# First cross attention of a two-layer decoder: rotation and values partly moved to ScalarE and GpSimd, gate and places made for pairs of batches

## The chip, the cores and the metric

The kernel runs on one core of a Trainium2 chip. The metric is the device time of one execution in microseconds. The engines are named as in the profile: PE (TensorE matmul) and PEld (its weight loads), DVE (VectorE), ACT (ScalarE), POOL (GpSimd), SP (SyncE, which here issues DMAs).

## The reference

A decoder of two layers with a layer norm after each of six parts works on `x` of shape (16, 128, 256), float32:

```python
x = ln(x + L0_attn(x));  x = ln(x + L0_xattn(x, ctx));  x = ln(x + L0_ffn(x))
x = ln(x + L1_attn(x));  x = ln(x + L1_xattn(x, ctx, ctx)); x = ln(x + L1_ffn(x))
```

The change lies in the second part, `L0_xattn`, and in the gate that leads to the third. The cross attention treats the 128 rows as channels and the 256 columns as positions, with 16 heads of 8 channels, of which 4 are rotated by position:

```python
q = rope(wq @ x + bq);  k = rope(wk @ c + bk);  v = wv @ c + bv      # per head
p = softmax(q @ k.T / sqrt(8));  out = wo @ (p @ v) + bo
```

The third part is a mixture of 8 experts, of which each row takes the two best:

```python
w = softmax(x @ Wg + bg);  topv, topi = top_k(w, 2)
out = sum over the two of topv * expert[topi](x)    # three matrix products, gelu between
```

## The kernel before

All of `x` stays in SBUF as 16 tiles `x_t[b]` of 128x256, one per batch. The ternary self attention (`ternary`) and the first cross attention (`rope_cross_plain`) form one stream, which `by_beats` writes out by hand. The cross attention has 8 beats per batch. In each beat PE makes a group of scores for the maxima (of one batch) and a group of transposed scores for the exponentials (of an earlier batch, 11 beats behind); then come the products with the values two beats later, and then the jobs of the beat. Where a job stands relative to its batch is in the list `jobs` as a number of beats.

What sets the order of the work: PE's instructions are kept in the order in which the program writes them (`mm` and `turned`, L216 to L222). On the other engines a scheduler chooses the order when the program is built, and each engine then runs its list in that order. So an engine that waits for one thing holds up all that stands behind it in its list.

Buffers in PSUM: the scores `ps_st` have three buffers in turn, the sums `ps_o` one, and everything else shares one buffer `ps_m` once the ternary attention has ended. Each `ps_st` for the maxima goes into the buffer that the last exponential (`pT`, L443 on ACT) has read.

A batch in the cross attention, by its jobs and lines:

- `keys` and `queries` (beats -8 and -5): PE makes two products into `ps_m`, the plain one and the one for the rotation. `rotated` (L766) makes `rot` (L770) and `rot_t` (L771) on DVE and adds them on POOL (L772). For the queries POOL then makes four masked copies `z` (L858).
- `values` (beat 5): two products, and DVE adds the bias `bv2` while it spreads them into `v8` (L871).
- maxima: DVE reduces the scores (`nm`, L438); the job `maxima` (beat 9) turns them on PE.
- `divide` (beat 20, L319 to L325): ACT copies the sums to `ol`, DVE shuffles the row sums into place (`l`, L322), ACT takes Ln and Exp for the reciprocal (L323, L324), DVE multiplies (L325).
- `finish` (beat 23): output product, bias and residual (L841), and the layer norm `normalised`, whose `rstd` is a power on POOL (L195).
- `gate_turn`, `gate`, `places` (beats 25, 26, 28): PE turns `x_t[b]` (L222), ACT copies it (`gate_xT`, L782); the gate's product, softmax, the two best (DVE, ACT); from these the place of each row in its experts' lists (counts so far in `free`), and two scatters of `x_t[b]` to `xs` in device memory by indirect DMA on POOL's queue (L831).

The experts (`experts_by_place`) then read `xs` in order, on SP's queue (`xe<-xs`, L943).

Of the kernel before, what the change touches and what calls it, by code (L numbers as in the profile page):

```python
# [9 lines left out]
F32 = mybir.dt.float32  # L10
# [19 lines left out]
def kernel(ctx: ExitStack, tc: tile.TileContext, a: dict, out: bass.AP):  # L30
# [11 lines left out]
    def load(pool, shape, src, name, dtype=F32, eng=None):  # L42
        t = pool.tile(shape, dtype, name=name)
        (eng or nc.sync).dma_start(t, src)
        return t
# [105 lines left out]


    xw = load(cpool, [P, 8, P], a["xw"], "xw", eng=nc.gpsimd)
    xb = load(cpool, [P, 5], a["xb"], "xb", eng=nc.gpsimd)
    bv2 = load(cpool, [P, D], a["bv2"].partition_broadcast(P), "bv2", eng=nc.gpsimd)
    rope = load(cpool, [P, 2, D], a["rope"], "rope", eng=nc.gpsimd)
    ctx_t = [load(cpool, [P, D], a["ctx"][b], f"ctx_{b}", eng=nc.gpsimd) for b in range(B)]
# [59 lines left out]
    def mm(*args, **kw):  # L217

        tc.keep_in_program_order(nc.tensor.matmul(*args, **kw))  # L219
# [93 lines left out]
        nc.vector.tensor_tensor(oT.rearrange("p c q -> p (c q)"), o[:, 0, :], r, ALU.mult)  # L313
        return oT

    def divided_pairs(pl, o):


        ol = pl["w"].tile([P, 2, D], F32, name="ol")  # L319
        nc.scalar.copy(ol, o)  # L320
        l = pl["w"].tile([P, 2, D], F32, name="l")
        nc.vector.stream_shuffle(l, ol, [n % 16 + 16 for n in range(32)])  # L322
        nc.scalar.activation(l, l, AF.Ln)  # L323
        nc.scalar.activation(l, l, AF.Exp, scale=-1.0)  # L324
        nc.vector.tensor_tensor(l, ol, l, ALU.mult)  # L325
        return l

    def rows_of(g):
        return slice(32 * g, 32 * g + 32)
# [436 lines left out]
    def rotated(pl, pab, n, dst):  # L766

        t0 = pl[dst].tile([P, D], F32, name=f"rot{n}")
        t1 = pl["w"].tile([P, D], F32, name="rot_t")
        nc.vector.scalar_tensor_tensor(t0, pab[:, 0, :], xb[:, 2 * n : 2 * n + 1], rope[:, 0, :], ALU.add, ALU.mult)  # L770
        nc.vector.scalar_tensor_tensor(t1, pab[:, 1, :], xb[:, 2 * n + 1 : 2 * n + 2], rope[:, 1, :], ALU.add, ALU.mult)  # L771
        nc.gpsimd.tensor_tensor(t0, t0, t1, ALU.add)  # L772
        return t0

# [2 lines left out]
    def gate_turn(pl, b):  # L777
        pt = pl["m"].tile([P, 2, P], F32, name="ps_m")
        for c in range(2):
            turned(pt[:, c, :], x_t[b][:, c * P : (c + 1) * P], ident)  # L780
        xT = pl["w"].tile([P, 2, P], F32, name="gate_xT")
        nc.scalar.copy(xT, pt)  # L782
        gates[b] = xT

    def gate(pl, b):

        xT = gates[b]
        pg = pl["m"].tile([P, 8], F32, name="ps_m")
        for c in range(2):
            mm(pg, lhsT=xT[:, c, :], rhs=wg[:, c, :], start=(c == 0), stop=(c == 1))  # L790
        gw = small.tile([P, 8], F32, name="gw")
        nc.vector.tensor_tensor(gw, pg, bg, ALU.add)
        gm = small.tile([P, 1], F32, name="gm")
        nc.vector.tensor_reduce(gm, gw, AX.X, ALU.max, negate=True)
        gs = small.tile([P, 1], F32, name="gs")
        nc.scalar.activation(gw, gw, AF.Exp, bias=gm, accum_out=gs)
        nc.vector.reciprocal(gs, gs)
        nc.vector.tensor_scalar_mul(gw, gw, gs)
        nc.vector.max(gv[:, b, :], gw)
        gi = small.tile([P, 8], U32, name="gi")  # L800
        nc.vector.max_index(gi, gv[:, b, :], gw)
        gf = small.tile([P, 2], F32, name="gf")
        nc.vector.tensor_copy(gf, gi[:, 0:2])
        nc.vector.tensor_tensor(
            oh[:, b], gf.unsqueeze(2).to_broadcast([P, 2, 8]), iota8.unsqueeze(1).to_broadcast([P, 2, 8]), ALU.is_equal
        )
        both = small.tile([P, 8], BF16, name="both")
        nc.vector.tensor_tensor(both, oh[:, b, 0, :], oh[:, b, 1, :], ALU.add)
        gates[b] = gf, both

    def places(pl, b):

        gf, both = gates.pop(b)
        pp = pl["m"].tile([P, 2, 8], F32, name="ps_m")
        mm(pp[:, 0, :], lhsT=above, rhs=both, start=True, stop=True)
        mm(pp[:, 1, :], lhsT=onesb, rhs=both, start=True, stop=True)
        at = small.tile([P, 8], F32, name="at")
        nc.vector.tensor_tensor(at, pp[:, 0, :], free[b % 2], ALU.add)
        nc.vector.tensor_tensor(free[(b + 1) % 2], pp[:, 1, :], free[b % 2], ALU.add)
        own_at = small.tile([P, 2, 8], F32, name="own_at")  # L820
        nc.vector.tensor_tensor(own_at, oh[:, b], at.unsqueeze(1).to_broadcast([P, 2, 8]), ALU.mult)
        pf = small.tile([P, 2], F32, name="place_f")
        nc.vector.tensor_reduce(pf, own_at, AX.X, ALU.add)

        past = small.tile([P, 2], F32, name="past")
        nc.vector.tensor_scalar(past, gf, float(NT - CAP), float(8 * CAP), ALU.mult, ALU.add)
        nc.vector.scalar_tensor_tensor(past, pf, float(CAP), past, ALU.is_ge, ALU.mult)
        nc.vector.scalar_tensor_tensor(pf, gf, float(CAP), pf, ALU.mult, ALU.add)
        nc.vector.tensor_tensor(place[:, b, :], pf, past, ALU.add)
        for n in range(2):  # L830
            nc.gpsimd.indirect_dma_start(  # L831
                out=xs[:, :], out_offset=bass.IndirectOffsetOnAxis(ap=place[:, b, n : n + 1], axis=0), in_=x_t[b],
                in_offset=None,
            )

    def cross_finish(pl, b, *products):
        po = pl["m"].tile([P, D], F32, name="ps_m")
        for n, (w, oT) in enumerate(products):
            mm(po, lhsT=xw[:, w, :], rhs=oT, start=(n == 0), stop=(n == len(products) - 1))
        xn = pl["w"].tile([P, D], F32, name="xn")  # L840
        nc.vector.scalar_tensor_tensor(xn, po, xb[:, 4:5], x_t[b], ALU.add, ALU.add)  # L841
        normalised(x_t[b], xn)

    def rope_cross_plain(pl):

        kept = {}

        def side(b, n, src):
            pab = pl["m"].tile([P, 2, D], F32, name="ps_m")
            for i in range(2):  # L850
                mm(pab[:, i, :], lhsT=xw[:, 2 * n + i, :], rhs=src, start=True, stop=True)
            return rotated(pl, pab, n, "wq"[n])

        def queries(b):
            q = side(b, 0, x_t[b])
            z = pl["q"].tile([P, 4, D], F32, name="z")
            for i in range(4):
                nc.gpsimd.tensor_scalar_mul(z[:, i, :], q, hm[:, 2 + i : 3 + i])  # L858
            kept[b]["qz"] = z

        def keys(b):
            kept[b] = {}
            kept[b]["k"] = side(b, 1, ctx_t[b])

        def values(b):
            pv = pl["m"].tile([P, 2, P], F32, name="ps_m")
            for kc in range(2):
                mm(pv[:, kc, :], lhsT=ctx_t[b][:, kc * P : (kc + 1) * P], rhs=xw[:, 4, :], start=True, stop=True)
            v = kept[b]["v"] = v8[b % 2]
            for n in range(2):  # L870
                nc.vector.tensor_tensor(  # L871
                    v[:, :, n::2, 8 * n : 8 * n + 8],
                    pv.rearrange("p c (g i n d) -> p (c g) i n d", g=4, i=2, n=2)[:, :, :, n, :],
                    bv2.rearrange("p (g i n d) -> p g i n d", g=8, i=2, n=2)[:, :, :, n, :], ALU.add,
                )

        def maxima(b):
            kept[b]["nmT"] = turned_maxima(pl, kept[b]["nm"], nmx[b % 2], 4)

        def divide(b):  # L880
            kept[b] = divided_pairs(pl, kept[b]["o"])

        def finish(b):
            oT = kept.pop(b)
            cross_finish(pl, b, (6, oT[:, 0, :]), (7, oT[:, 1, :]))

        jobs = [(20, divide), (9, maxima), (-8, keys), (-5, queries), (5, values), (23, finish),
                (25, lambda b: gate_turn(pl, b)), (26, lambda b: gate(pl, b)), (28, lambda b: places(pl, b))]
        return 8, 11, cross_scores(pl, 16, kept, 11), jobs, range(B)

    def rope_cross_masked(st):
# [3 lines left out]
        for b in range(B):  # L895
# [16 lines left out]
            v = v8p[b % 2]  # L912
            nc.vector.tensor_copy(own_channels(v, 16), vn.rearrange("p c (h d) -> p c h d", h=16))
            oT = cross_heads(pl, 16, rot[0], [z[:, i, :] for i in range(4)], v, dict(masked, v=vn))
            cross_finish(pl, b, (5, oT.rearrange("p c q -> p (c q)")))
            for part in (gate_turn, gate, places):
                part(pl, b)

# [109 lines left out]


    most1 = const.tile([P, 1], F32, name="most1")  # L1030
    nc.vector.tensor_reduce(most1, free[B % 2], AX.X, ALU.max)
    most_i = const.tile([P, 1], I32, name="most_i")
    nc.vector.tensor_copy(most_i, most1)
    fullest = nc.values_load(most_i[0:1, 0:1], min_val=0, max_val=NT)
# [417 lines left out]
def layouts(inputs):  # L1452
# [20 lines left out]
    for n in range(2):  # L1473
# [9 lines left out]
        "rope": rope.astype(np.float32),  # L1483
        "w0": np.stack([i[f"L0_attn_w_{n}"].T for n in "qkvo"], 1),
        "xw": np.stack([wq.T, wq[mate].T, wk.T, wk[mate].T, wv.T, wo.T] + pairs, 1),
        "xb": np.stack([bq, bq[mate], bk, bk[mate], bo], 1),
        "bv2": np.concatenate([i["L0_xattn_bv"]] * 2),
        "wg": i["L0_ffn_Wg"],
        "bg": i["L0_ffn_bg"],
# [41 lines left out]
```

## Time and profile before

| | |
|---|---|
| median of 3 runs | 1535.75 us (1534.78 to 1538.27) |
| profiled execution, own time | 1539.54 us |
| its span, first to last instruction | 1537.8 us |
| PE busy, PE weight loads | 1372.2 us (89%), 857.4 us (56%) |
| DVE, ACT, POOL busy | 814.4 (53%), 568.0 (37%), 271.6 us (18%) |
| first cross attention alone | from about 200 to 565 us |
| granted TensorE clock, mean | 0.959 |

The times are medians of whole executions; the profile is one execution, and its span is what sums from its rows are held against. Busy time is counted per engine from the records. A matmul's end is modelled, so a busy PE may still have gaps. In a timeline row the first number is the start, the second the duration in us, then engine, line, operation, output and inputs; in brackets stands how long the engine was idle before it and which instruction ended that wait. In a row of waits stand the total in us, how often, and the longest.

### The profile page before, as it was taken

Reading aid. Unit: us, or ns where it says so; the run is one execution under the profiler, and the core shown is the slowest. Engines: PE = TensorE matmul, PEld = TensorE weight load, DVE = VectorE, ACT = ScalarE, POOL = GpSimd, SP = SyncE. Lnnn points to the kernel's source line nnn. Section 1 sums busy time; section 2 is a strip of 40 time slices with the busy share of each in tenths; the row PEclk is TensorE's granted clock in tenths of the full one; section 3 lists DMA queues with packets and bytes.
Section 4 is the critical chain, followed back from the end, with each engine's and each line's share of the span. In section 5 each row is a group of like instructions: output and inputs, shape, how many; then the busy total and the mean of one; then the engine's idle time right before and its main releaser. Section 6 shows DMA issues by size and latency. Waiting matters only on the chain. (4 is left out here: it accounts for less than half of the span.)

```text
span 1537.8 us, 28608 instructions
## 1 busy us (share of the span) xinstructions
PE 1372.2 (89%) x12011; PEld 857.4 (56%) x12011; DVE 814.4 (53%) x2258; ACT 568.0 (37%) x955; POOL 271.6 (18%) x372
## 2 busy tenths in 40 slices
PE   4999989989998949999999679889899998999997
PEld 3666544445444427777777456556455544446666
DVE  6788867777787530000000147766666656542322
ACT  1444334454445512111111124434455554762110
POOL 7000323433333110000000133321122100000000
PEclk9999979999999969999999859989999998999999
DMA  9200000000000025322220411100000000000000
GB/s 298 74 2 2 2 1 8 15 12 12 15 15 12 15 92 168 98 90 89 94 67 18 145 39 29 29 1 2 1 2 1 2 1 1 1 1 12 17 7 20
DMA packets 41743, 58.14 MB, mean 38 GB/s; under 512 B 4752, under 2 KB 31392, under 8 KB 41472
## 3 DMA queue, kind: packets, MB, share of 16 engines
q1 hardware_dynamic: 35984, 41.95, 8.3%
q0 software_dynamic: 4784, 13.42, 2.7%
q8 instruction: 98, 1.61, 0.4%
q10 hardware_dynamic: 832, 0.79, 0.2%
q14 instruction: 45, 0.37, 0.1%
HBM read 39.37 MB, written 16.78 MB: 37 GB/s over the span
## 5 line engine op out<-in xcount | busy, mean ns | idle before, releaser
L438 DVE TENSOR_REDUCE nm<-ps_st 128x4 f32<-128x1024 f32 x192 | 233.7, 1220 | 85.1 <-PE ps_st L219 84.5
L443 ACT ACTIVATE pT<-ps_st 128x1024 f32<-128x1024 f32 x192 | 196.3, 1023 | 212.0 <-PE ps_st L219 212.0
L195 POOL TENSOR_TENSOR rstd<-ve,nhalf 128x1 f32<-128x1 f32 x112 | 62.6, 559 | 681.8 <-DVE ve L194 665.6
L219 PE MATMUL ps_st<-rot,z 32*128 32x256 f32 x1024 | 149.4, 410 | 26.4 <-ACT pT L443 24.0
L219 PE MATMUL ps_o<-pT,v 128*32 128x256 f32 (+1 forms) x2560 | 164.8, 347 | 1.0 <-DVE oT L313 0.8
L977 DVE TENSOR_TENSOR ye<-ps_e,b 128x256 f32<-128x256 f32 x40 | 17.0, 425 | 265.8 <-PE ps_e L974 265.8
L962 PE MATMUL ps_h<-h,w 128*128 128x320 f32 x512 | 139.1, 432 | 0.0
L966 ACT ACTIVATE h<-ps_h,b 128x640 f32<-128x640 f32 x64 | 50.8, 794 | 228.6 <-PE ps_h L962 228.5
L219 PE MATMUL ps_st<-z,rot 32*128 32x512 f32 x512 | 132.6, 596 | 0.0
L219 PE MATMUL ps_st<-nmT,pick 32*128 32x256 bf16 x1024 | 112.1, 277 | 10.4 <-ACT nmT L304 7.4
L962 PEld LDWEIGHTS ps_h<-h,w 128*128 128x128 f32 x512 | 97.3, 190 | 40.5
L219 PEld LDWEIGHTS ps_st<-rot,z 32*128 32x128 f32 x1024 | 89.9, 188 | 42.1 <-ACT pT L443 31.9
L219 PEld LDWEIGHTS ps_o<-pT,v 128*32 128x32 f32 x2560 | 55.1, 109 | 99.7 <-issue 87.6
L375 DVE TENSOR_REDUCE nm<-ps_st 128x8 f32<-128x1024 f32 x64 | 78.1, 1220 | 35.9 <-PE ps_st L219 33.7
L1073 POOL DMA_INDIRECT y<-ys,place x32 | 31.1, 972 | 314.0 <-DMA ys<-ye 306.3
L219 PEld LDWEIGHTS <-pick 32*128 32x128 bf16 x1024 | 36.1, 91 | 80.3 <-issue 73.7
L219 PE MATMUL ps_o<-pT,ones 128*32 128x256 f32 x1024 | 79.1, 381 | 0.0
L962 PE MATMUL ps_h<-xeT,w 128*128 128x320 f32 x256 | 73.7, 447 | 2.2 <-DMA w<-in_W_dram 1.1
L219 PE MATMUL ps_st<-ctx,z 32*128 32x256 f32 x512 | 72.1, 398 | 0.5 <-DVE nm L438 0.4
L974 PE MATMUL ps_e<-w,h 128*128 128x256 f32 x320 | 70.4, 379 | 0.0
L219 PE MATMUL ps_f<-fxT,fgw 128*128 128x512 f32 x128 | 62.7, 613 | 6.7 <-ACT g L1249 6.7
L974 PEld LDWEIGHTS ps_e<-w,h 128*128 128x128 f32 x320 | 60.8, 190 | 9.1
(279 smaller groups left out, 2467.5 us busy)
## 6 DMA issues: line engine op xcount, KB each, us to landing
w<-in_W_dram SPq DMA_DIRECT2D x16, 512.0 KB, 4.0
w<-in_W_dram SPq DMA_DIRECT2D x8, 1024.0 KB, 5.4
xs<-zero SPq DMA_DIRECT2D x40, 128.0 KB, 4.2
xe<-xs SPq DMA_DIRECT2D x40, 128.0 KB, 3.6
ys<-ye SPq DMA_DIRECT2D x40, 128.0 KB, 2.0
x<-in_x_dram SPq DMA_DIRECT2D x16, 128.0 KB, 7.4
ctx<-in_ctx_dram POOLq DMA_DIRECT2D x16, 128.0 KB, 5.2
out_dram<-x SPq DMA_DIRECT2D x16, 128.0 KB, 1.7
```

What stands on the lines that cost most here:

```text
L195: in_order(nc.gpsimd.tensor_tensor(dst, ve, nhalf, ALU.pow))
L219: tc.keep_in_program_order(nc.tensor.matmul(*args, **kw))
L375: nc.vector.tensor_reduce(zs["nm"].rearrange("p c g n -> p g c n")[:, gs : gs + 2], ps, AX.X, ALU.max, negate=True)
L438: nc.vector.tensor_reduce(zs["nm"][:, qc, gs : gs + 2, js : js + 2], ps, AX.X, ALU.max, negate=True)
L443: nc.scalar.activation(pT, pt, AF.Exp)
L962: nc.tensor.matmul(ps[:, n, 0:H], lhsT=w[:, c, hc * P : (hc + 1) * P], rhs=src[:, c, n * H : (n + 1) * H], start=(c == 0), stop=(c == part ...
L966: nc.scalar.activation(dst[:, hc, :].rearrange("p (n t) -> p n t", n=2), ps[:, :, 0:H], AF.Gelu, bias=b12[:, layer, e, hc : hc + 1],)
L974: nc.tensor.matmul(ps, lhsT=h2[:, fc, c * P : (c + 1) * P], rhs=w3[:, fc, :], start=(fc == 0), stop=(fc == 3))
L977: nc.vector.tensor_add(ye[:, c, :], ps, b3[:, e, :])
L1073: in_order(nc.gpsimd.indirect_dma_start(out=y, out_offset=None, in_=ys[:, :], in_offset=bass.IndirectOffsetOnAxis(ap=place[:, b, n : n + 1 ...
```

## The change

Four things change in the cross attention and the gate. The job `divide` is split into three jobs in consecutive beats (copy and shuffle, reciprocal, product). The values no longer get their bias; instead the output weights times that bias, computed once, are added to the output bias, and ACT instead of DVE copies the values. The second operand of the rotation is made by ACT (bias) and POOL (product with the table) instead of DVE. Gate and places run once for two batches, in the beats of the second one: the even batch does only its `gate_turn`, and the odd one makes the gate's products, the choice, the places and the four scatters of both.

```diff
-    xb = load(cpool, [P, 5], a["xb"], "xb", eng=nc.gpsimd)
+    xb = load(cpool, [P, 6], a["xb"], "xb", eng=nc.gpsimd)
...
-    def divided_pairs(pl, o):
+    def pair_sums(pl, o):
         ol = pl["w"].tile([P, 2, D], F32, name="ol")
         nc.scalar.copy(ol, o)
         l = pl["w"].tile([P, 2, D], F32, name="l")
         nc.vector.stream_shuffle(l, ol, [n % 16 + 16 for n in range(32)])
+        return ol, l
+
+    def reciprocals(l):
         nc.scalar.activation(l, l, AF.Ln)
         nc.scalar.activation(l, l, AF.Exp, scale=-1.0)
-        nc.vector.tensor_tensor(l, ol, l, ALU.mult)
-        return l
...
-        nc.vector.scalar_tensor_tensor(t1, pab[:, 1, :], xb[:, 2 * n + 1 : 2 * n + 2], rope[:, 1, :], ALU.add, ALU.mult)
+        nc.scalar.activation(t1, pab[:, 1, :], AF.Identity, bias=xb[:, 2 * n + 1 : 2 * n + 2])
+        nc.gpsimd.tensor_tensor(t1, t1, rope[:, 1, :], ALU.mult)
         nc.gpsimd.tensor_tensor(t0, t0, t1, ALU.add)
...
     def gate(pl, b):
+        if b % 2 == 0:
+            return
+        two = slice(b - 1, b + 1)
+        xT = gates[b // 2]
+        pg = pl["m"].tile([P, 2, 8], F32, name="ps_m")
+        for k in range(2):
+            for c in range(2):
+                mm(pg[:, k, :], lhsT=xT[:, k, c, :], rhs=wg[:, c, :], start=(c == 0), stop=(c == 1))
...
+        for k in range(2):
+            nc.scalar.activation(gw[:, k, :], gw[:, k, :], AF.Exp, bias=gm[:, k : k + 1], accum_out=gs[:, k : k + 1])
...
+        for k in range(2):
+            nc.vector.max(gv[:, b - 1 + k, :], gw[:, k, :])
+            nc.vector.max_index(gi[:, k, :], gv[:, b - 1 + k, :], gw[:, k, :])
...
     def places(pl, b):
+        if b % 2 == 0:
+            return
...
+        mm(pp[:, 0:2, :], lhsT=above, rhs=both, start=True, stop=False)
+        mm(pp[:, 1, :], lhsT=onesb, rhs=both[:, 0, :], start=False, stop=False)
+        for n in range(2):
+            mm(pp[:, 2, :], lhsT=onesb, rhs=both[:, n, :], start=False, stop=(n == 1))
...
-        for n in range(2):
-            nc.gpsimd.indirect_dma_start(
-                out=xs[:, :], out_offset=bass.IndirectOffsetOnAxis(ap=place[:, b, n : n + 1], axis=0), in_=x_t[b],
-                in_offset=None,
-            )
+        for c in (b - 1, b):
+            for n in range(2):
+                nc.gpsimd.indirect_dma_start(
+                    out=xs[:, :], out_offset=bass.IndirectOffsetOnAxis(ap=place[:, c, n : n + 1], axis=0), in_=x_t[c],
+                    in_offset=None,
+                )
...
+        def biases(b):
+            if b:
+                return
+            pb = pl["m"].tile([P, 1], F32, name="ps_m")
+            mm(pb, lhsT=xw[:, 5, :], rhs=xb[:, 5:6], start=True, stop=True)
+            bias_of["ov"] = const.tile([P, 1], F32, name="bias_ov")
+            nc.vector.tensor_tensor(bias_of["ov"], pb, xb[:, 4:5], ALU.add)
...
-                nc.vector.tensor_tensor(
+                nc.scalar.copy(
                     v[:, :, n::2, 8 * n : 8 * n + 8],
                     pv.rearrange("p c (g i n d) -> p (c g) i n d", g=4, i=2, n=2)[:, :, :, n, :],
-                    bv2.rearrange("p (g i n d) -> p g i n d", g=8, i=2, n=2)[:, :, :, n, :], ALU.add,
                 )
...
-        jobs = [(20, divide), (9, maxima), (-8, keys), (-5, queries), (5, values), (23, finish),
+        jobs = [(20, sums_out), (21, invert), (22, divide), (9, maxima), (-9, biases), (-8, keys), (-5, queries), (5, values), (23, finish),
                 (25, lambda b: gate_turn(pl, b)), (26, lambda b: gate(pl, b)), (28, lambda b: places(pl, b))]
```

## The prediction

> **What bounds the kernel now.** I read the slices of the page first (PE at nine tenths from end to end, but POOL and the clock dip where the first cross attention begins and ends), then the windows by stage, then the waits of each engine between 240 and 520 us (thirteen blocks of the stage), then the timeline of one block.
>
> The stage runs at 21.86 us per batch (the projections of `x` start at 314.21, 336.14 and 357.97 us). PE sets that pace. Its named waits in the thirteen blocks are these:
>
> ```profile
> PE ps_st L219 <- ACT pT L443: 20.9, 41, 0.9
> PE ps_m L222 <- ACT gate_xT L782: 6.7, 13, 0.5
> ```
>
> That is 1.6 and 0.5 us per block, and no wait on VectorE among them. VectorE is 76% busy there but never late for PE. The windows say the same (columns: PE, PEld, DVE, ACT, POOL busy, then the granted clock):
>
> ```profile
> 180.00:200.00 20.00, 16.77 (x130) 10.07 (x128) 16.82 (x38) 2.10 (x6) 5.58 (x7) 0.80 0.00 1
> 200.00:220.00 20.00, 17.98 (x152) 9.74 (x148) 13.64 (x26) 6.14 (x6) 5.45 (x7) 0.77 0.00 1
> ...
> 300.00:320.00 20.00, 18.86 (x212) 10.18 (x204) 15.55 (x44) 9.65 (x14) 6.26 (x8) 1.00 0.04 15
> ```
>
> The first two rows are where the ternary attention ends and the cross attention starts: there VectorE is the bound, and the clock is down.
>
> The largest wait of a block is where the division falls (timeline, one block):
>
> ```profile
> 339.52 0.58 ACT L320 COPY ol<-ps_o 128x512 f32<-128x512 f32 x1
> ...
> 340.90 0.63 ACT L323 ACTIVATE l<-l 128x512 f32<-128x512 f32 x1 [0.80 <-DVE place_f L823]
> ...
> 342.10 1.01 ACT L443 ACTIVATE pT<-ps_st 128x1024 f32<-128x1024 f32 x1
> ...
> 343.15 0.48 PE L219 MATMUL ps_st<-rot,z 32*128 32x256 f32 x2 [0.90 <-ACT pT L443]
> ```
>
> ScalarE copies the sums, waits for VectorE's shuffle (340.14 to 340.87), runs Ln and Exp, and only then the next `pT`; PE, which needs that score buffer back, waits 0.90.
>
> The view that decides this case is GpSimd's queue in the same block:
>
> ```profile
> 338.88 0.72 POOL L772 TENSOR_TENSOR rot<-rot,rot_t 128x256 f32<-128x256 f32 x1 [7.26 <-DVE rot_t L771]
> 339.71 4.00 POOL L858 TENSOR_SCALAR z<-rot,hm 128x256 f32<-128x256 f32 x4
> 343.87 1.06 POOL L831 DMA_INDIRECT xs<-x,place  x1 [0.17 <-issue]
> 346.65 0.97 POOL L831 DMA_INDIRECT xs<-x,place  x1 [1.72 <-DMA xs<-x,place]
> 349.71 0.57 POOL L195 TENSOR_TENSOR rstd<-ve,nhalf 128x1 f32<-128x1 f32 x1 [2.08 <-DVE ve L194]
> ```
>
> The second scatter waits until the first has landed: 2.77 us from start to start. Behind both stands the `rstd` of the next batch's layer norm, and behind that:
>
> ```profile
> 350.31 0.41 DVE L205 TENSOR_SCALAR x<-xn,mv,rstd 128x256 f32<-128x256 f32 x1 [0.57 <-POOL rstd L195]
> ...
> 352.73 0.44 PE L222 MATMUL ps_m<-ident,x 128*128 128x128 f32 x2
> ```
>
> PE turns that `x` 2.0 us after it is there. PE takes its work in order, so these 2.0 us are all the room.
>
> **The change, part by part.** I take each engine's order from the two programs.
>
> *Three steps.* In the changed program ScalarE still has `ol`, Ln, Exp and then `pT`: the steps were put in later beats, but the order came out as before. VectorE has the shuffle and then the product, as before. The shuffle already starts 0.04 after `ol` ends (340.10), so a freer VectorE cannot start Ln earlier. Gain 0; the 0.90 stays.
>
> *Bias of the values.* Two VectorE additions of 0.28 us per batch go, two ScalarE copies come. No row has a 128x128 copy on ScalarE; 128x8 takes 0.30, 128x256 0.37, so 0.33 each. They stand after the `pT` of 342.10 and end near 343.8; the next `pT` starts at 344.36. Cost 0, hidden by ScalarE's wait for PE; were that gone, 0.7 per block. The new matrix product for the bias is one of 12,011, and the sixth column of `xb` rides in a load that is there already; SP's queue issues nothing else.
>
> *Rotation.* Two VectorE operations of 0.476 per batch become two on ScalarE (nearest row 0.37, `gate_xT`, same shape and source; at least the 0.30 of eight columns, at most the 0.58 of 512) and two on POOL (0.72 each, the row of L772). ScalarE's stand between two `pT` with 1.8 us idle ahead of them; POOL gets 1.45 per batch and waits longer for its inputs (107 us in thirteen blocks). Cost 0 here.
>
> *Gate for two batches.* A block without gate gains nothing: the 0.55 of its matrix products (333.77 to 334.31) ends 0.17 before PE would wait for `pT` anyway, and without it the wait is longer. A block with gate has eight products instead of four: +0.55 less the 0.17, so **+0.38**. On VectorE the chain grows by one more Exp with accumulation (0.39), MAX8 and FIND_INDEX8 (0.42) and wider shapes, about 0.9; the reduces and the rotation stand behind it in the order, less one 0.40 saved, so the shuffle starts about 0.57 late against PE, and Ln, Exp and `pT` with it: **+0.57**.
>
> *Places for two batches.* Four scatters in a row on POOL, in every second block, each with a wait for the one before, and `rstd` behind all four. Worked out in the times above, for such a block: the rotation on VectorE ends at 339.72, POOL adds until 340.5, `z` until 344.6, the scatters start at 344.75, 347.5, 350.3 and 353.1; `rstd` 354.1 to 354.7 instead of 349.71; `x` done at 355.1. On VectorE stand behind this `x`, in the order, a reduce (1.22) and the rotation of the keys (0.47) that frees the only `ps_m` buffer: 356.7. PE wants that buffer for turning `x` at 352.73 + 0.95 = 353.68. PE idles **3.05 us**. Late next is nothing more: `nm` is done by 356.3, before PE needs it.
>
> A block with gate so costs 0.38 + 0.57 + 3.05 = 4.0. There are five (places of pairs up to batch 9): 20.0. For batches 10 and 11 no keys' rotation follows: 0.95 + 1.5 = 2.5.
>
> *The end.* For batches 12 and 13 the scatters start near 534.8 and end near 544.2, so batch 14's `rstd` comes at 544.3 instead of 540.67 and PE turns its `x` 2.2 late. Then the last pair:
>
> ```profile
> 560.69 0.96 POOL L831 DMA_INDIRECT xs<-x,place  x1 [5.63 <-DVE place L829]
> 563.36 0.96 POOL L831 DMA_INDIRECT xs<-x,place  x1 [1.72 <-DMA xs<-x,place]
> ```
>
> The experts' first load follows at 566.25. Batch 14's scatters lay under other work; now all four stand here: 2 x 2.67 = 5.3. The gate ahead of them is 2.0 longer (four products at the low clock 1.0, Exp 0.4, VectorE 0.4, places 0.2). Sum 9.5.
>
> *The start.* At 188.5 to 190.2 PE waits 1.65 for a reduce that sits in VectorE's backlog; about 0.4 to 0.8 of it goes with the rotation. I take -2.
>
> *The clock.* A stall can cost more than its length. After that wait of 1.65, the trace has matrix products at half speed (2.08 instead of 1.13) from 191.8 to about 209. The Trainium skill, "TensorE: Matmul & The Clock Gate", section "HAM oscillation", says that idle gaps of over about 3.4 us are what has to be avoided. By that rule 3.05 would cost nothing more, and the sum would be 20 + 2.5 + 9.5 - 2 = +30. By this trace 1.65 was enough. I go by the trace. For the length of a slow spell I have this one of 17 us and the page's own figure (section "Part 1: The HAM clock gate") of one busy window of about 3.4 us; I estimate one and a half such windows, as PE is full there. At half speed a beat of 2.73 takes about 4.5 (body 2 x 1.6, job 2 x 0.65), so a window loses 1.3. Five times 2.0: **+10**.
>
> Sum 20 + 2.5 + 9.5 - 2 + 10 = +40 against the profiled span of 1537.8 (own time 1539.54). The median is 1535.75, 3.8 below; set on it, **1576**.
>
> **Rivals.**
> *A, the forecast*: 1567 to 1588. Chance 0.47.
> *B, stalls without clock loss* (the page's rule holds): +30 or somewhat less, 1556 to 1567. For it: most of PE's short waits of up to 0.9 leave the clock at 1.00. Chance 0.20.
> *C, long slow spells*: each stall brings four or five windows as at 191.8. 5 x 6 = 30 instead of 10: about 1596, up to 1605. Against: there PE was short of work, here it isn't. Chance 0.16.
> *D, the scatters are absorbed*: if they follow each other at 2.0 us or less, `x` is in time. Then 6 x 0.95 + 2 + 4 - 2, about +10: 1546. Against: 2.67 or more in every block. Chance 0.08.
> *E, faster*: VectorE's lateness is what makes ScalarE late. The trace names VectorE (`place_f`) as releaser of Ln in 13 blocks, 10.7 us. If the lighter VectorE lets Ln and Exp run ahead, the 20.9 of PE's waits go, and the start keeps its clock (-7). With +10 for the end and +3 for the gate: 1535.75 - 15, about 1521. It decides only if the scatters come at 2.0 or less too, since otherwise +18 and the clock stand against it; and the shuffle's start 0.04 after `ol` speaks against it. Chance 0.07.
> *No change* (gains and losses cancel): 0.02.
>
> **The numbers.** 0.2%, or 3 us, is about what a measurement of this kernel can tell from no change. Slower: A to D, 0.91. Same 0.02, faster 0.07. The range 1550 to 1602 holds A, B and most of C, with scatter spacing, stall and clock at their bounds.
>
> **What would show it.** In the profile after: in every second block four DMA_INDIRECT about 2.77 apart, `rstd` behind them, PE's `ps_m<-ident,x` waiting 2 to 3.5 us, and none in the blocks between, which should keep 21.9. Five dips of the clock between 250 and 520. ScalarE's Ln right behind `ol`. The experts' first load about 10 us later against the last `ol`. Wrong if `rstd` runs before the scatters, if they don't wait for each other, or if every block is shorter than 21.5.

## The result, and the profile after

The changed kernel takes 1593.45 us (median of four runs, 1591.49 to 1597.35) against 1535.26 for the kernel before in the same comparison: ratio 1.038, 95% interval 1.0353 to 1.0408. That is 58 us slower, inside the range given and on the forecast side, but 17 us beyond the forecast. The profiled execution took 1597.35 (span 1595.6), 3.9 above the median, just as the profile of before stood 3.8 above its own.

All of it is lost in the first cross attention. The experts' first load starts at 624.66 us instead of 566.25, +58.4; behind it both traces run alike (row of before, then of after):

```profile
566.25 0.80 SPq L943 DMA_DIRECT2D xe<-xs  x2
624.66 1.75 SPq L975 DMA_DIRECT2D xe<-xs  x4
```

In some runs of four experiment kernels below, the mean granted clock is about 0.01 lower and the time 8 to 20 us longer; a median that holds such runs is marked.

The waits between 240 and 560 us (engine, tile and line, what it waited for: us in total, times, longest) show the new wait of PE at the top of its list:

```profile
DVE x L205 <- POOL rstd L195: 36.0, 13, 6.5
POOL xs L847 <- DMA xs<-x,place: 34.4, 18, 3.5
...
PE ps_m L222 <- ACT rot_t L772: 23.0, 5, 5.9
PE ps_st L219 <- ACT pT L444: 21.4, 39, 0.9
...
PE ps_m L222 <- ACT gate_xT L785: 8.3, 13, 0.7
...
PE ps_m L222 <- DVE x L205: 4.5, 1, 4.5
```

Six waits, 27.5 us, for the tile `ps_m` or for `x` itself: one for every pair whose scatters stand ahead of an `rstd` in the steady part. PE's wait for `pT`, which the three steps were to take away, has stayed at 0.9. One block with four scatters, from the timeline of after (start, duration, engine and line, operation, and in brackets the idle time before it and what ended it):

```profile
380.87 0.59 ACT L320 COPY ol<-ps_o 128x512 f32<-128x512 f32 x1
...
382.25 0.63 ACT L326 ACTIVATE l<-l 128x512 f32<-128x512 f32 x1 [0.80 <-DVE l L322]
...
383.45 1.01 ACT L444 ACTIVATE pT<-ps_st 128x1024 f32<-128x1024 f32 x1
...
384.51 0.48 PE L219 MATMUL ps_st<-rot,z 32*128 32x256 f32 x2 [0.90 <-ACT pT L444]
...
386.08 1.06 POOL L847 DMA_INDIRECT xs<-x,place  x1 [0.17 <-issue]
...
388.84 0.98 POOL L847 DMA_INDIRECT xs<-x,place  x1 [1.71 <-DMA xs<-x,place]
...
391.55 0.96 POOL L847 DMA_INDIRECT xs<-x,place  x1 [1.73 <-DMA xs<-x,place]
...
394.22 0.96 POOL L847 DMA_INDIRECT xs<-x,place  x1 [1.71 <-DMA xs<-x,place]
395.20 0.59 POOL L195 TENSOR_TENSOR rstd<-ve,nhalf 128x1 f32<-128x1 f32 x1
395.82 0.41 DVE L205 TENSOR_SCALAR x<-xn,mv,rstd 128x256 f32<-128x256 f32 x1 [4.74 <-POOL rstd L195]
397.28 0.47 DVE L771 SCALAR_TENSOR_TENSOR rot<-ps_m,xb,rope 128x256 f32<-128x256 f32 x1
397.85 0.47 ACT L772 ACTIVATE rot_t<-ps_m,xb 128x256 f32<-128x256 f32 x1 [5.99 <-DVE rot L771]
398.38 0.69 PE L222 MATMUL ps_m<-ident,x 128*128 128x128 f32 x2 [4.23 <-ACT rot_t L772]
```

Read from below: PE stood 4.23 us because `ps_m` was still to be read by ScalarE; ScalarE had been idle for 5.99 and was let in only when VectorE's `rot` was done; VectorE had stood 4.74 for `rstd`; and `rstd` was behind four scatters, 2.71 us apart on average. The turn of `x` then runs at half speed (0.69 instead of 0.44). The windows (columns as before: PE, PEld, DVE, ACT, POOL, then the granted clock) show the dip around it:

```profile
370.00:380.00 10.00, 8.94 (x102) 4.88 (x97) 6.69 (x20) 5.16 (x12) 1.45 (x2) 1.00 0.01 2
380.00:390.00 10.00, 8.19 (x94) 4.71 (x97) 7.09 (x16) 6.00 (x10) 7.63 (x8) 1.00 0.04 15
390.00:400.00 10.00, 5.28 (x54) 2.59 (x50) 4.15 (x12) 2.71 (x5) 3.96 (x5) 0.85 0.11 39
400.00:410.00 10.00, 9.57 (x96) 5.00 (x96) 4.88 (x6) 4.36 (x6) 2.27 (x3) 0.80 0.01 2
```

Six such dips lie between 294 and 558 us, each of 6.8 us. At the end of the stage the last pair's four scatters stand alone, from 613.87 to the load at 624.66:

```profile
613.87 1.03 POOL L847 DMA_INDIRECT xs<-x,place  x1 [8.18 <-DVE place L844]
616.61 0.97 POOL L847 DMA_INDIRECT xs<-x,place  x1 [1.71 <-DMA xs<-x,place]
619.45 0.96 POOL L847 DMA_INDIRECT xs<-x,place  x1 [1.87 <-DMA xs<-x,place]
622.12 0.96 POOL L847 DMA_INDIRECT xs<-x,place  x1 [1.71 <-DMA xs<-x,place]
```

### The profile page after: what moved, and what is told of

Its sections match the earlier page's. It is cut to its first block, busy times and chain, and to the rows that moved or that the text cites. A ratio compares the mean times of both kernels' runs of the same rounds, so it can differ in the third digit from the quotient of the medians.

```text
span 1595.6 us, 28577 instructions
## 1 busy us (share of the span) xinstructions
PE 1386.2 (87%) x12013; PEld 862.4 (54%) x12013; DVE 782.4 (49%) x2075; ACT 586.0 (37%) x1019; POOL 291.3 (18%) x404
## 5 line engine op out<-in xcount | busy, mean ns | idle before, releaser
L219 PE MATMUL ps_st<-rot,z 32*128 32x256 f32 x1024 | 158.2, 429 | 27.5 <-ACT pT L444 25.8
L219 PE MATMUL ps_o<-pT,v 128*32 128x256 f32 (+1 forms) x2560 | 168.8, 355 | 1.0 <-DVE oT L313 0.8
L219 PE MATMUL ps_st<-z,rot 32*128 32x512 f32 x512 | 140.1, 627 | 0.0
L219 PEld LDWEIGHTS ps_st<-rot,z 32*128 32x128 f32 x1024 | 94.7, 199 | 44.4 <-ACT pT L444 34.0
L222 PE MATMUL ps_m<-ident,x 128*128 128x128 f32 x96 | 22.9, 325 | 51.0 <-DVE x L205 27.5
```

The lines of the kernel that those rows point to most:

```text
L222: tc.keep_in_program_order(nc.tensor.transpose(out, src, identity))
```

## The experiments

The theory from the two profiles: the pairing makes the loss, by four scatters ahead of one `rstd`, by ScalarE's late read of `ps_m` on top, and by the fall of the clock. The rivals: the new work on ScalarE and GpSimd; the pair's longer gate chain; PE's own work. "Changed kernel" is the one of the diff above. The kernel before had medians of 1535.26 to 1536.45 in all comparisons.

**Without the pairs** (`e1_no_pairs`): the changed kernel, `gate` and `places` as before.

```diff
-        for c in (b - 1, b):
-            for n in range(2):
+        for n in range(2):
...
-            mm(pg[:, k, :], lhsT=xT[:, k, c, :], rhs=wg[:, c, :], start=(c == 0), stop=(c == 1))
+            mm(pg, lhsT=xT[:, c, :], rhs=wg[:, c, :], start=(c == 0), stop=(c == 1))
```

> The changed kernel with gate and places for one batch at a time, as before; the three-step division, the values' bias through the output weights and the half rotation on ScalarE and GpSimd are kept. Theory (the loss comes from the pairing alone): every block has two scatters again, rstd is no longer late, PE's wait for rot_t of 4.2 us and the six dips of the clock in the steady blocks are gone. Left are what the changed kernel's even blocks showed, +0.35 us each over 14 blocks, and about +1 at the start: 1535 + 6 = about 1541 us, 1536 to 1545. Rival (the new work on ScalarE and GpSimd is what slows the stage, its queue being longer): most of the +58 stays, 1575 or more. Second rival (the lighter VectorE helps once the pairs are gone): under 1532.

Measured: 1553.76 (ratio 1.0127, 1.0095 to 1.016); three of the six runs are those with a lower clock, the others took 1549.0 to 1549.6. The waits of 4 us and the dips are gone, so the pairing does make most of the loss. But about 13 us stay, where I expected 6. From block to block the lag behind the kernel before grows by 0.76 us (turn of `x`: +2.79 at the second, +11.12 at the thirteenth): something in the other three parts costs, in every block.

**Pairs alone** (`e2_pairs_only`): the kernel before, with the diff of `gate_turn`, `gate` and `places` and nothing else.

```diff
-        for n in range(2):
+        for c in (b - 1, b):
+            for n in range(2):
...
+        if b % 2 == 0:
+            return
```

> The kernel before with the gate and places of two batches taken together and nothing else changed; the rotation stays whole on VectorE and the values' bias is added there. Theory (stall = scatters in a row, lengthened by ScalarE's rot_t waiting for VectorE's rot): four scatters 2.77 apart and rstd behind them as in the changed kernel; PE's wait per odd block is shorter by the ScalarE step, 3.0 to 3.9 instead of 4.2, two windows of half speed (6.8 us, worth 2.5) after each; tail +10. Sum 6 x (3.5 + 2.5 + 1) + 10 = +52: about 1587 us, 1578 to 1594. Rival (rotation and copies on the other engines carry a good part of the loss): under 1570.

Measured: 1581.15 (1.0275, 1.0248 to 1.0301), as expected. PE's wait for `ps_m` is 18.2 us over five, 3.6 each, where the changed kernel has 4.6. Without what scatters that landed late add to single waits, it is 3.2 against 4.2. The rotation makes that difference: the first of the four scatters starts 8.1 us after the projection of the next `x` here, and 9.2 after it in the changed kernel, where GpSimd has one product more ahead of them and its input comes from ScalarE's later read. +45 here and +13 to +17 in the run before make up the +58.

**Scatters in a later beat** (`e3_scatter_later`):

```diff
-        for c in (b - 1, b):
-            ...
+        scatter(b - 1)
...
-                (25, lambda b: gate_turn(pl, b)), (26, lambda b: gate(pl, b)), (28, lambda b: places(pl, b))]
+                (25, lambda b: gate_turn(pl, b)), (26, lambda b: gate(pl, b)), (28, lambda b: places(pl, b)), (36, scatter_second)]
```

> The changed kernel, with the pair's gate and places still together, but the scatters of the second batch issued eight beats later, so that rstd of the next batch stands behind two scatters and not four. Theory: the waits of 4.2 us and the dips of the clock in the steady blocks vanish; what is left is the pair's longer gate (about +1 per pair), the start (+1) and the end, where all four scatters of the last pair still stand alone (+8 to 10): 1545 to 1555 us. Rival (the longer gate chain and PE's order, not the scatters, make the pair slow): the loss stays over half, 1565 or more.

Measured: 1595.89 (1.0395, 1.0373 to 1.0417), no gain. Its timeline says why: the four scatters still stand in a row (382.26, 385.03, 387.72, 390.39) and `rstd` behind them at 391.37. The beat in which a job is written does not set GpSimd's order, any more than it did for Ln and Exp on ScalarE. The run tells nothing on the theory; it is a second measurement of the changed kernel.

**Scatters behind `rstd`** (`e5_scatter_after_rstd`): the same, and the order stated.

```diff
-        in_order(nc.gpsimd.tensor_tensor(dst, ve, nhalf, ALU.pow))
+        power = nc.gpsimd.tensor_tensor(dst, ve, nhalf, ALU.pow)
+        if keep:
+            tc.keep_in_program_order(power)
...
-            nc.gpsimd.indirect_dma_start(
+            tc.keep_in_program_order(nc.gpsimd.indirect_dma_start(
```

> As the run with later scatters, but now the order of rstd and the scatters on GpSimd is fixed: at most two scatters stand between one rstd and the next, in every block, while gate and places are still made for two batches at once. Theory: PE's wait of 4.2 us and the two windows of half speed after it go, six times 6.7 = 40 off the changed kernel's 1593; what is left above the kernel before is the rotation's share (the run without pairs had +17) and the last pair's four scatters: 1553 to 1562. Rival (the pair's longer gate chain, late shuffle and rot_t make the loss, four scatters or not): 1575 or more.

Measured: 1554.72 (1.0117, 1.0088 to 1.0147), 39 us below the changed kernel. GpSimd's timeline now has two scatters to a block:

```profile
368.39 1.06 POOL L854 DMA_INDIRECT xs<-x,place  x1 [0.17 <-issue]
371.15 0.97 POOL L854 DMA_INDIRECT xs<-x,place  x1 [1.70 <-DMA xs<-x,place]
373.37 0.57 POOL L195 TENSOR_TENSOR rstd<-ve,nhalf 128x1 f32<-128x1 f32 x1 [1.25 <-DVE ve L194]
...
389.75 1.06 POOL L854 DMA_INDIRECT xs<-x,place  x1 [0.18 <-issue]
392.52 0.97 POOL L854 DMA_INDIRECT xs<-x,place  x1 [1.71 <-DMA xs<-x,place]
395.57 0.57 POOL L195 TENSOR_TENSOR rstd<-ve,nhalf 128x1 f32<-128x1 f32 x1 [2.07 <-DVE ve L194]
```

`rstd` waits for VectorE again and not for scatters; no dip of the clock is left between 203 and 558 us. A pair of blocks lags by 1.7 us, against 7.8 in the changed kernel: 6.1 is the price of four scatters in one row. Gate and places for two batches, taken for themselves, cost 0.2 (1.7 less twice the 0.76 of the run without pairs).

**Filling PE's idle time, at the wrong place** (`e4_filled`) **and at the right one** (`e6_filled`): the keys' product is computed again so that PE works where it would idle; the result is unchanged.

```diff
-            for i in range(2):
+            again = 3 if n == 1 and b >= 5 and b % 2 else 0         # e4
+            again = 2 if n == 1 and b >= 4 and b % 2 == 0 else 0    # e6
+            for i in [1] * 2 * again + [0, 1]:
```

> The changed kernel; in every second block from batch 5 on, one of the products of the keys' projection is computed four times instead of once (six more 128x256 products, about 1.3 us at full speed; the result is the same), and these stand just ahead of PE's wait for ps_m. They shorten the idle stretch without moving anything that PE waits for. Theory (an idle stretch of 4.2 costs its length and two windows of half speed on top, 2.5 us): the stage's length is set by rstd in these blocks, so the extra products cost nothing, and where the shorter idle stretch keeps the clock at full speed 2.5 us per block are won back: five blocks, down to about 1581 us. If a shorter idle stretch of 2.9 still drops the clock, nothing changes: 1593. Rival (PE, not the wait, sets the pace; the loss is in the longer work): five times 1.3 or more slower, 1600.

> The filling of PE's idle stretch at the right place: one product of the keys' projection of every even batch from 4 on is computed three times (four more 128x256 products, in two passes each: 8 x 0.28 = 2.3 us at full speed), just ahead of PE's wait for ps_m in the block with four scatters; the result is the same. The wait shrinks from 4.2 to about 2, the end of the wait stays where rstd puts it. Theory (the idle stretch drops the clock for two windows, 2.5 us on top): if 2 us of idling leave the clock alone, five or six dips vanish and the time falls by some 12, to 1581; if 2 us are enough to drop it, 1593 to 1597. Rival (PE's own work sets the pace in these blocks): 2.3 x 6 slower, 1607.

Measured for the first: 1611.54 (1.049, 1.0467 to 1.0514). I had the parity wrong: the keys of odd batches are computed in the blocks without a wait. The run is 18 us above the changed kernel. In the trace each of the six blocks with the products is 2.4 longer than there, 14.6 in all (scatters that landed late add some 5, and an earlier start of the blocks takes 4.5 off). That is what PE's work costs where PE sets the pace.

Measured for the second: 1600.9 (1.0424, 1.0395 to 1.0453). Its timeline:

```profile
393.66 2.86 PE L219 MATMUL ps_m<-ctx,xw 128*128 128x256 f32 x12
...
398.21 0.41 DVE L205 TENSOR_SCALAR x<-xn,mv,rstd 128x256 f32<-128x256 f32 x1 [4.72 <-POOL rstd L195]
...
400.76 0.69 PE L222 MATMUL ps_m<-ident,x 128*128 128x128 f32 x2 [2.49 <-ACT rot_t L772]
...
403.50 1.06 PE L219 MATMUL ps_st<-z,rot 32*128 32x512 f32 x2
```

PE's wait has shrunk to 2.49 here (2.60 and 2.50 in the two other blocks whose scatters landed on time), and its end has not moved (21.5 us behind the projection of `x`, as in the changed kernel): `rstd` sets it. The clock falls all the same (1.06 instead of 0.59), now wholly under work: for 3.4 to 6.8 us after the waits of about 2.5, for up to 10.2 after longer ones. So 2.5 us of idling were enough here. The time lies between the 1593 to 1597 that I expected in that case and the rival's 1607, and the run can't price the clock.

**The rotation alone** (`e7_rotation_only`) **and with ScalarE reading first** (`e11_scalar_first`), on the kernel before:

```diff
-        nc.vector.scalar_tensor_tensor(t1, pab[:, 1, :], xb[:, 2 * n + 1 : 2 * n + 2], rope[:, 1, :], ALU.add, ALU.mult)
+        nc.scalar.activation(t1, pab[:, 1, :], AF.Identity, bias=xb[:, 2 * n + 1 : 2 * n + 2])
+        nc.gpsimd.tensor_tensor(t1, t1, rope[:, 1, :], ALU.mult)
```

In `e11_scalar_first` the first of the new lines stands ahead of VectorE's line for `t0`.

> The kernel before with one part of the change: the second half of the rotation goes by ScalarE (bias) and GpSimd (product). Theory (ScalarE's rot_t is let in only after VectorE's rot, though both only read the same PSUM tile, so the tile comes free later and ScalarE's next operations start later): PE waits 0.2 more for gate_xT, 0.1 to 0.3 more for pT and some 0.15 at the turn, about 0.75 per block as in the run without pairs: 14 x 0.75 = +10, 1543 to 1553 us. Rival (the +17 of the run without pairs comes from the values' copies on ScalarE): within 3 us of 1536. A gain from the lighter VectorE: under 1533.

> The rotation alone again, with the two readers of the PSUM tile in the other sequence in the program: ScalarE's bias first, VectorE's product second. Theory (the second reader is made to wait for the first, whatever the engines): VectorE's rot now waits for ScalarE's rot_t; ScalarE stands idle for 1.8 us there and can read as soon as the projection is done, while VectorE is still at a reduce, so the tile comes free after VectorE's one operation of 0.48 instead of its two of 0.87; the 0.75 per block is gone and up to 0.3 is won: 1530 to 1538 us. Rival (the cost is the work on ScalarE itself, not the sequence): 1544 as before.

Measured for the first: 1544.17 (1.0045, 1.0026 to 1.0064), and a lag of 0.76 per block, the same as without pairs. The rotation is the part that costs. Its timeline:

```profile
337.27 0.47 DVE L770 SCALAR_TENSOR_TENSOR rot<-ps_m,xb,rope 128x256 f32<-128x256 f32 x1
...
337.85 0.47 ACT L771 ACTIVATE rot_t<-ps_m,xb 128x256 f32<-128x256 f32 x1 [1.73 <-DVE rot L770]
338.22 1.02 ACT L443 ACTIVATE pT<-ps_st 128x1024 f32<-128x1024 f32 x1
...
339.29 0.48 PE L219 MATMUL ps_st<-rot,z 32*128 32x256 f32 x2 [0.51 <-ACT pT L443]
```

ScalarE idled 1.73 us and then read, behind VectorE, just when its next `pT` was due; PE waits 0.51 for that `pT` where it waited 0.29, then 1.03 where it was 0.90, and 0.73 for `gate_xT` where it was 0.51. These are 0.57 of the 0.76.

Measured for the second: 1532.33 (0.9972, 0.996 to 0.9984), 12 us below the first:

```profile
321.25 0.47 ACT L770 ACTIVATE rot_t<-ps_m,xb 128x256 f32<-128x256 f32 x1 [0.63 <-PE ps_m L219]
...
321.89 0.47 DVE L771 SCALAR_TENSOR_TENSOR rot<-ps_m,xb,rope 128x256 f32<-128x256 f32 x1
...
322.84 0.44 PE L222 MATMUL ps_m<-ident,x 128*128 128x128 f32 x2
```

Now ScalarE reads as soon as PE is done, and its work is over before `pT` is due. The same operations on the same engines cost 0.76 per block or nothing, by the order of two reads. The blocks are as long as before (lag -7.84 at the first turn, -8.20 at the thirteenth), so the further 0.3 per block that I hoped for did not come; the small gain lies ahead of them. In this trace the slow spell at the stage's start lasts 6.8 us instead of 17.1, which would fit, but a single trace can't show it.

**The values' bias alone** (`e9_values_only`):

```diff
-                nc.vector.tensor_tensor(
+                nc.scalar.copy(
...
-                    bv2.rearrange("p (g i n d) -> p g i n d", g=8, i=2, n=2)[:, :, :, n, :], ALU.add,
```

> The kernel before with one part of the change: the values' bias goes through the output weights into the bias of the sum, and ScalarE copies the values where VectorE added the bias. The run without pairs took 9 us more than the run with the rotation alone, though its blocks are as long in the two profiles (0.76 us per block over the kernel before in both). Theory (the copies lie in ScalarE's idle time behind a pT and cost nothing in the steady blocks; the 9 us lie ahead of them, at the stage's start): blocks as before, 21.87, and a time between 1536 and 1545. Rival (the copies delay a pT and cost in each block): 0.3 x 14 or more, with longer blocks.

Measured: 1541.93 (1.0038, 1.002 to 1.0056; two of 15 runs are those with a lower clock). The blocks are as before to 0.05 us over all (lag -1.88 at the first turn, -1.84 at the thirteenth), as the theory has it; where the 3 us (without those two runs) to 6 us are lost is left open. With the rotation's 8 they make up about the 13 of the run without pairs. The profiled execution took 1538.48, a microsecond less than the profile of before, and shows no place for it.

**The three steps alone, in order** (`e8_steps_in_order`): the kernel before with the split of `divided_pairs`, and ScalarE's order stated.

```diff
+        tc.keep_in_program_order(nc.scalar.copy(ol, o))
...
+        tc.keep_in_program_order(nc.scalar.activation(l, l, AF.Ln))
+        tc.keep_in_program_order(nc.scalar.activation(l, l, AF.Exp, scale=-1.0))
...
-                nc.scalar.activation(pT, pt, AF.Exp)
+                tc.keep_in_program_order(nc.scalar.activation(pT, pt, AF.Exp))
...
-        jobs = [(20, divide), (9, maxima)
+        jobs = [(20, sums_out), (21, invert), (22, divide), (9, maxima)
```

> The kernel before with the division in three steps alone, and with ScalarE's order fixed so that the steps take place in their own beats: copy of the sums, the next pT, and only then Ln and Exp. Theory (the three steps did nothing because ScalarE's order came out as before; PE's 0.90 for the pT behind Ln and Exp is real): that wait goes from every block, 14 x 0.9 = 12.6 less, and no other takes its place because ScalarE has 1.8 us idle later in the block: 1522 to 1528 us. Rival (the wait only moves to the next pT, behind which Ln and Exp now stand, or to VectorE's product): 1532 to 1538.

Measured: 1517.65 (0.9871, 0.9845 to 0.9898), 19 us faster than the kernel before and 76 faster than the changed one. The timeline:

```profile
333.01 0.58 ACT L320 COPY ol<-ps_o 128x512 f32<-128x512 f32 x1
...
334.43 1.02 ACT L444 ACTIVATE pT<-ps_st 128x1024 f32<-128x1024 f32 x1 [0.84 <-PE ps_st L219]
...
335.35 0.62 ACT L326 ACTIVATE l<-l 128x512 f32<-128x512 f32 x1
...
335.51 0.48 PE L219 MATMUL ps_st<-rot,z 32*128 32x256 f32 x2
```

`pT` goes ahead of Ln and Exp, and PE's product at 335.51 has no wait where it had 0.90. A block takes 20.7 us instead of 21.87, 1.2 less: the 0.90, 0.05 of the wait for `gate_xT`, and 0.25 that no named wait shows.

**The whole change with both orders stated** (`e10_orders_fixed`), and **the two helpful parts** (`e12_steps_scalar_first`: steps in order, and the rotation with ScalarE first, on the kernel before); both are sums of the diffs above.

> The whole change with both orders put right: on GpSimd at most two scatters between one rstd and the next, on ScalarE pT ahead of Ln and Exp. Theory (the two orders add up, being on different engines and in different beats): 1554.7 less the 18.8 that the fixed steps were worth to the kernel before, 1536, within 1532 to 1542; so the rest of the change (pairs, rotation, values) is worth +18 whatever the order of the steps. Rival (rot_t and the values' copies fill the room on ScalarE that the steps need): 1545 or more.

> The kernel before with the two parts that could help: division in three steps with ScalarE's order fixed, and the rotation's second half by ScalarE, read first. Theory: 1517.6 less what the sequence of the readers wins in the run beside this one, 1511 to 1518. Rival (ScalarE's rot_t now stands ahead of a pT that PE waits for): 1520 to 1526.

Measured: 1540.75 (1.0049, 1.0018 to 1.008; three of 11 runs with a lower clock), so the two orders together are worth 53 of the 58 us, and what else the change does still costs more than the steps bring. Its trace shows where: from the first turn of `x` to the fourteenth the blocks gain 2.8 us on the kernel before (lag -2.80, then -5.62), and the end, with the four scatters that stand alone, loses 6.9 (the experts' first load comes at 567.52, +1.3). The second: 1520.7 (0.9902, 0.9876 to 0.9927); its two runs with a lower clock took 1530 and 1534, the other four 1517.1 to 1522.6. That is the steps' gain and nothing on top. No version measured here is faster than the plainest: the steps in order alone.

## Why the prediction was right or wrong

The direction, the place and the main mechanism held: four scatters some 2.7 apart, `rstd` behind them, PE waiting for `ps_m`, the clock falling after each wait. In the sum, several sizes were off, and one term, the rotation, was put at nothing and was not; that the total still lies in the range is in part because too large terms (gate, clock) stand against too small ones. Both traces, by the turns of `x` and the projections:

| term | forecast | in the trace |
|---|---|---|
| start | -2 | +0.9 |
| pairs, places up to batch 9 | 5 x 6.0 | 5 x 7.8 |
| pair 10/11 | 2.5 | 7.9 |
| end | 9.5 | 10.3 |
| sum | +40 | +58 |

*Start.* Not to be judged: over the profiles here the first turn of `x` lies anywhere between 235.5 and 246.5, and 4.5 us apart in two kernels that are the same up to there (the changed kernel 244.4, `e4_filled` 239.9).

*Three steps, gain 0.* Right, and for the reason given: ScalarE's order came out as before. The 0.90 was real, though, and 19 us could have been had.

*Rotation, cost 0.* This step failed. I took 1.8 us of idle time ahead of ScalarE's operation as its cover. But that idle time ends where VectorE's read ends: the second reader of a PSUM tile was let in after the first, and then it stood in front of a `pT`. That is 0.76 per block, 1.5 per pair. And in the blocks with a wait both new steps stand on the path to `ps_m` and to the scatters, which adds some 1.0 to the stall (below): 2.5 of a pair's 7.8. The operation takes 0.47 besides, not the 0.37 of the nearest row, and VectorE, which it was to ease, is busy for 78% of the blocks' time, not 76%. The waits of before, over the whole span, could have told me:

```profile
ACT v L1128 <- DVE k L1126: 40.3, 16, 5.0
```

In the later latent attention ScalarE copies `v` out of one half of a tile of which VectorE copies `k` out of the other, no data pass between them, and ScalarE waits 2.5 us each time.

*Gate pair, 0.95.* Too large: 0.2 by the run with scatters behind `rstd`. Held against the rotation alone, its blocks with a gate lose 0.39 between the turn of `x` and the next projection, as forecast (0.38), and 0.2 behind it instead of 0.57; but a block without gate and places, which was to gain nothing, gains 0.45.

*Stall, 3.05.* Too small: 4.6 on average (27.5 us over six). Where the scatters landed on time PE waits 4.2 to 4.35, 1.2 more than worked out. Counted from the projection of the next `x` (336.14 in the prediction's block), `rstd` starts at 18.35 and not at 17.96: the prediction names GpSimd's new product of 0.72, but its chain to the scatters has only the addition. From `rstd` to the turn of `x` it is 3.2 and not 2.6, as ScalarE's read stands behind VectorE's (in the block above VectorE's ends at 397.75, ScalarE's at 398.32). And PE is ready 0.25 sooner. The rest of the average are two waits in which scatters landed 1.7 and 1.8 late (5.94, and the pair of 10 and 11). Why they land late there, the runs do not show.

*Batches 10 and 11, 2.5.* Wrong for this kernel: PE waited 4.5 us for `x` itself, and the clock fell as in the other pairs. The reason given, that no keys' rotation follows and the wait is short, held in the pairs alone, where PE waits 1.80 (1.5 worked out). In the changed kernel the scatters start 1.1 later, and the last had to wait 3.53 for the one before:

```profile
549.26 0.96 POOL L847 DMA_INDIRECT xs<-x,place  x1 [3.53 <-DMA xs<-x,place]
```

*Clock, 5 x 2.0.* The prediction chose between the rule of the Trainium skill ("TensorE: Matmul & The Clock Gate", section "HAM oscillation": idle gaps of over about 3.4 us are to be avoided) and the 1.65 of its trace. The changed kernel's waits of over 4 pass both marks. The filled kernel shows the rule's mark to be too high here: the clock was halved after waits of 2.49, 2.50 and 2.60. But the 1.65, from a stretch where PE was short of work, was too low a mark for full work. In the pairs alone PE waited 1.80 for the `x` of batch 12, and the granted clock stayed at 1.00:

```profile
536.36 0.44 PE L222 MATMUL ps_m<-ident,x 128*128 128x128 f32 x2 [1.80 <-DVE x L205]
535.00:539.00 4.00, 2.18 (x28) 1.26 (x28) 2.83 (x4) 1.03 (x4) 0.84 (x2) 1.00 0.09 33
```

So to go by the trace gave the right answer, with a mark that doesn't hold in these blocks. The spell was two windows of 3.41 us and not one and a half, yet its price was smaller. From the turn of `x` to the next projection, blocks with a wait lose 1.8 us (2.50, 1.35, 1.60, 1.76, 1.78); the same blocks in the run with scatters behind `rstd`, which has no dip, lose 0.2. That makes 1.6 per pair. A part of each spell lies in the wait, where a slow clock costs nothing.

So a pair's 7.8 is 4.6 of waiting, 1.5 of rotation, 1.6 of clock and 0.2 of gate, to 0.1.

*The end, 9.5.* Close: 2.65 at the turn of batch 14 (2.2 worked out), 6.8 from the last `ol` to the experts' load (7.3 worked out), and 0.8 between the two that was not in the sum.

Rival C, long slow spells, gives about the right number (1596) for a reason that did not occur: no spell of the changed kernel's steady part exceeded two windows. Rival B's premise fell, since waits did cost clock. D and E fell with the scatters' spacing and ScalarE's order.

## What to carry to other kernels

Before an operation is costed at nothing because its engine is idle there, look at what ends that idle time: an engine that waits for another reader of the same tile has no room. Putting a job into a later beat changes nothing until each queue's order is read, or stated; here one stated order turned a part worth nothing into 19 us, and another took 39 us off. Batching small work for fewer instructions also batches its transfers, and what stands behind them in the queue pays.

## What the runs showed of the hardware

- After an idle stretch of 4.2 to 5.9 us in otherwise full work, PE's clock was halved for 6.8 us, twice the shortest spell seen (3.41), in all six cases of the changed kernel. After 2.49, 2.50 and 2.60 us it still fell, for 3.4 to 6.8; after 1.80 us, in one case, it did not.
- Near the end of a stage, where work thins out, the clock can fall earlier in one execution than in another: in the profiled one of the steps with ScalarE first it came at 508 us and lasted 64.9, against 534 and 27.3 for the steps alone, and the run took 13 us more than the median of its kernel. Only this one trace shows such a fall; for the other runs with a lower mean clock, its place is not known.
- A ScalarE operation of 0.47 us, with the GpSimd product behind it, cost 0.76 us per block or nothing, by whether it read its PSUM tile behind VectorE or ahead of it.
- A scatter on GpSimd's queue started 2.7 us after the one before, 1.7 of it waiting for that one to land; in single cases this wait was 2.2 to 3.6.
